# A transformer block with self- and cross-attention on one core: VectorE's remainders and statistics spread one to a beat, reciprocals of even units two beats later, the split of the contexts' keys on GpSimd

## The chip, the cores and the metric

The kernel runs on one NeuronCore of one Trainium2 chip. Five engines take part, each with its own in-order queue: TensorE (PE; PEld is its weight load), VectorE (DVE), ScalarE (ACT), GpSimd (POOL) and SyncE (SP), which here only issues DMAs. The metric is the device time of one execution in microseconds (us). A difference of 0.2% is about what a measurement of this kernel can tell.

## The reference

A block with 16 heads of 16 channels is computed for 16 batches of 256 tokens, width 256, in float32. Each batch has a condition vector and a context of 256 tokens.

```python
x_norm = modulate(_ln(x), shift_a, scale_a)
q, k, v = split(x_norm @ W_qkv + b_qkv)              # 16 heads of 16
x = x + gate_a * (softmax(q k^T * scale) v @ W_proj + b_proj)
q_c = _ln(x) @ W_qc + b_qc
k_c, v_c = split(_ln(context) @ W_kvc + b_kvc)
x = x + softmax(q_c k_c^T * scale) v_c @ W_cproj + b_cproj
x_norm2 = modulate(_ln(x), shift_m, scale_m)
x = x + gate_m * (gelu(x_norm2 @ W_mlp1 + b_mlp1) @ W_mlp2 + b_mlp2)
```

## The kernel before

**Units.** The attention is done in 32 units, one after the other. A spatial unit s*b* is the self-attention of batch *b*, a context unit c*b* its cross-attention. Units 0 to 4 are s0 to s4; then they alternate, s5, c0, s6, c1, up to s15 and c10 (units 5 to 26), so that odd units are spatial and even ones are contexts; units 27 to 31 are c11 to c15. The MLP of all batches follows.

**Beats.** A unit takes 8 beats, one for each pair of head groups (`beat(n, k)`, k from 0 to 7). In each beat PE makes the scores `s` of unit n+1 (4 matmuls into the two banks of `s`), DVE takes their row maxima (`mxs<-s`, one TENSOR_REDUCE of 128x1024), PE makes the transposed scores `st` of unit n, and ACT takes their exponential (`pt<-st`). There is one buffer of `s`: the next beat's `s` matmuls wait for this beat's reduce. Between these four steps, the beats carry the preparation of later units and the rest of earlier ones. All engines keep the order in which the program is written (`InOrder`, L51; every instruction has this line in the profile).

**What is prepared.** Matmuls work on float32 values split into a high part and a remainder. For the unit n+2 (`q2` in the code) the keys `K` and the queries `Q` are finished in beats 0 and 4: ACT writes the high part (`h_k`, `h_q`; `h_kc`, `h_qc` for contexts) from the PSUM tile, DVE the remainder (`l_k`, `l_q`, `l_kc`, `l_qc`: two instructions of 128x256, one for each half f), and SP sends both to where the scores read them (`big`), the high part in two DMAs and the remainder in one, 256 KB each. For the unit n+4 the layer norm is made: `stats` (two bn_stats, `st_s` or `st_c`), `rstd` (two bn_aggr on DVE, `mv`, then two short POOL instructions, `rs`) and `apply` (two POOL instructions, `xn`). For the unit n+3 (`q3`) the normalized tokens are transposed (`psT`) and projected.

**What is finished.** The unit n-1 (`p1`) has its sums `S` pulled (SP), inverted (`recip`, DVE), written to DRAM (`spread`: `rd<-S`) and read back broadcast (`back`: `R<-rd`); POOL multiplies in beat 0 of the next unit (`norm`, `U`), splits the product (`xTh_a`, `xTl_a`), and PE projects it (`ps_P`) in beats 3 and 5.

**The three banks `tr`.** Five or six PSUM tiles of a unit share three banks (the tag `tr` in `ps_gen`). They are asked for in this order: `ps_q` (queries of n+2) and `psT` (tokens of n+3) in beat 1, the output tile `o` of the first half in beat 2, `ps_k` or `ps_kc` (keys of n+3) in beat 5, in beat 5 also a second `psT_q` where unit n+3 is a context (its queries come from the updated x), and `o` of the second half in beat 6. A tile gets a bank when the last reader of an earlier tile is done: for `ps_q` this is the remainder `l_q` on DVE, for `psT` of beat 1 an instruction of beat 3, for `o` the copy to `oT` on ACT (in beat 5, and in beat 0 of the next unit). The first matmul into the new tile waits for that reader.

**Beat 5 on PE.** Written order: `s` with the first pieces of `psT_q` between its halves, `st`, then the key projection of n+3 (`ps_kc`) and the output projection (`ps_P`) in turn, matmul by matmul, each on one half of the array's rows; then the next beat's `s`. This happens 16 times with a `psT_q`: in units 3, 5, ... 23, where the unit n+2 is spatial, and in units 24 to 28, where it is a context.

Of the kernel before, what the change touches and what calls it, by code (L numbers as in the profile page):

```python
# [10 lines left out]
F32 = mybir.dt.float32  # L11
F32R = mybir.dt.float32r
# [9 lines left out]
def pixart_block(  # L22
# [488 lines left out]
    def to_stack(W, src, bias, dst, which, name):  # L511
# [24 lines left out]
        def low():  # L536
            if name == "k0":
                gap(work, 64, "gap_l")
            o.lo = work.tile([P, KC, N], F32R, tag="qkl", name=f"l_{name}", bufs=3)
            if name == "k0":  # L540
                gap(work, 576, "gap_mx")
            for f in range(KC):
                DVE.scalar_tensor_tensor(o.lo[:, f], o.ps[:, f * N:(f + 1) * N], bias[f], o.hi[:, f],
                                         ALU.add, ALU.subtract)
# [609 lines left out]
    def spare(n, gate=True):  # L1154
        p1, _, p3 = (v and v.post for v in map(unit, (n - 1, n - 2, n - 3)))
        if p3 and not p3.added:
            p3.add()
        if p1 and gate:
            p1.gate()

    def beat(n, k):
# [11 lines left out]
        late = lc and lc.b in (0, B - 1)  # L1173
        if k == 0 and q2:
            q2.K.high()
            q2.K.send_high()
# [27 lines left out]
        if k == 0:  # L1204
# [6 lines left out]
            if q2:  # L1211
                q2.K.low()
                q2.K.send_low()
# [4 lines left out]
        elif k == 1:  # L1218
# [6 lines left out]
            if lx:  # L1225
                if lx.b in (0, B - 1):
                    lx.ln[1].steps[0]()
                lx.ln[1].steps[1]()
                lx.ln[1].steps[2]()
        elif k == 2:  # L1230
# [7 lines left out]
            if ls:  # L1238
                ls.ln[0].steps[0]()
            elif prev:  # L1240
                p1.recip()
                p1.spread()
            if not (q3 and q3.kind == "c"):
                spare(n)
        elif k == 3:
# [12 lines left out]
            if q3 and q3.kind == "s":  # L1258
                q3.T[0].low()
            if prev and ls:  # L1260
                p1.recip()
                p1.spread()
            if lx and n == nu - 4:
                lx.T[0].parts[2]()
        elif k == 4:
# [5 lines left out]
            if q2:  # L1271
                q2.Q.low()
                q2.Q.send_low()
# [4 lines left out]
            if ls:  # L1278
                ls.ln[0].steps[1]()
                ls.ln[0].steps[2]()  # L1280
                ls.ready = True
        elif k == 5:
# [4 lines left out]
            if lc:  # L1287
                lc.ln[0].steps[1]()
                lc.ln[0].steps[2]()
                lc.ready = True  # L1290
# [147 lines left out]
```

## Time and profile before

| what | value |
|---|---|
| median of 3 runs | 725.73 us (725.42 to 726.89) |
| the profiled execution | 722.92 us |
| its span, first to last instruction | 721.1 us |
| first and last row maximum (`mxs<-s`) of the 32 units | 18.9 and 524.2 us |
| one row maximum, 128x1024 | 1221 ns, 252 of them |
| mean granted TensorE clock | 1.000 |

The profile of one execution gives the busy time of each engine, waits (who waited for whom), groups of like instructions with the mean duration of one, and a timeline whose rows read: start in us, duration in us, engine, line, operation, tile written and tiles read, partitions x elements, number of instructions in the row, and in brackets the engine's idle time before the row with what ended it. Matmuls are pipelined and their ends are modelled, so rows of PE overlap and a busy PE may be waiting in part.

### The profile page before, as it was taken

Reading aid. Unit: us, or ns where it says so; the run is one execution under the profiler, and the core shown is the slowest. Engines: PE = TensorE matmul, PEld = TensorE weight load, DVE = VectorE, ACT = ScalarE, POOL = GpSimd, SP = SyncE. Lnnn points to the kernel's source line nnn. Section 1 sums busy time; section 2 is a strip of 40 time slices with the busy share of each in tenths; the row PEclk is TensorE's granted clock in tenths of the full one; section 3 lists DMA queues with packets and bytes.
Section 4 is the critical chain, followed back from the end, with each engine's and each line's share of the span. In section 5 each row is a group of like instructions: output and inputs, shape, how many; then the busy total and the mean of one; then the engine's idle time right before and its main releaser. Section 6 shows DMA issues by size and latency. Waiting matters only on the chain.

```text
span 721.1 us, 23569 instructions
## 1 busy us (share of the span) xinstructions
PE 704.2 (98%) x9359; PEld 600.5 (83%) x9359; DVE 566.5 (79%) x895; ACT 551.0 (76%) x956; POOL 520.5 (72%) x519
## 2 busy tenths in 40 slices
PE   9999999999999999999999999999999999999997
PEld 8777788788877878787778787877779999999997
DVE  5878888988888888778888888888765777777753
ACT  5677888888888888787888888877867677676661
POOL 7665778886776768676686698987766988676552
PEclk9999999999999999999999999999999999999999
DMA  7465455354545536454545556545332223223122
GB/s 238 166 201 200 151 185 194 134 182 167 176 161 186 177 138 189 160 177 150 184 164 193 172 186 204 166 153 206 102 104 87 89 59 89 69 66 86 48 59 74
DMA packets 82921, 106.22 MB, mean 147 GB/s; under 512 B 18970, under 2 KB 45916, under 8 KB 82812
## 3 DMA queue, kind: packets, MB, share of 16 engines
q1 hardware_dynamic: 81916, 104.37, 44.0%
q8 instruction: 74, 1.21, 0.8%
q10 hardware_dynamic: 896, 0.35, 0.2%
q14 instruction: 35, 0.29, 0.1%
HBM read 35.89 MB, written 8.98 MB: 62 GB/s over the span
## 4 chain that ended last, share of the span: by engine, by line
PE 75%; DVE 13%; DMA 4%; issue 2%; POOL 2%; SPq 2%; ACT 1%; POOLq 0%; ACTq 0%; DVEq 0%
PE s L51 18%; PE st L51 13%; PE ph L51 12%; PE o L51 10%; DVE mxs L51 9%; PE ps_kc L51 3%; PE ps_q L51 3%; PE ps_P_s L51 2%; PE ps_k L51 2%; PE ps_v_c L51 2%; SPq L51 2%; PE ps_qc L51 2%; DMA x<-in_x_dram 2%; PE ps_v_s L51 1%; DMA U_s<-oT 1%
## 5 line engine op out<-in xcount | busy, mean ns | idle before, releaser
L51 DVE TENSOR_REDUCE mxs<-s 128x4 f32<-128x1024 f32 x252 | 307.6, 1221 | 65.3 <-PE s L51 60.0
L51 ACT ACTIVATE pt<-st 128x1024 f32<-128x1024 f32 x256 | 262.6, 1026 | 74.6 <-PE st L51 70.4
L51 PE MATMUL s<-big 63*128 63x256 f32 x1008 | 132.9, 322 | 10.9 <-DVE mxs L51 4.3
L51 PE MATMUL o<-pt,v 128*32 128x256 f32 x2048 | 141.6, 384 | 0.0
L51 PEld LDWEIGHTS s<-big 63*128 63x128 f32 x1008 | 82.4, 185 | 70.4 <-DVE mxs L51 62.3
L51 PE MATMUL st<-big 64*128 64x256 f32 (+1 forms) x1040 | 112.4, 285 | 0.3 <-ACT pt L51 0.2
L51 PE MATMUL ph<-xTh_m,wself 128*128 128x256 f32 x512 | 99.6, 280 | 0.0
L51 POOL TENSOR_TENSOR hl<-hf,hh 128x512 fp32r<-128x512 f32 x60 | 80.2, 1354 | 19.2 <-ACT hh L51 19.2
L51 PEld LDWEIGHTS st<-big 64*128 64x128 f32 (+1 forms) x1040 | 85.7, 186 | 3.0 <-ACT pt L51 1.4
L51 PEld LDWEIGHTS o<-pt,v 128*32 128x32 f32 x2048 | 67.0, 109 | 21.7
L51 PEld LDWEIGHTS ph<-xTh_m,wself 128*128 128x128 f32 x512 | 81.9, 188 | 1.2 <-issue 0.4
L51 PE MATMUL ph<-xTl_m,wself 128*128 128x256 f32 x256 | 70.9, 277 | 0.0
L51 ACT ACTIVATE hf<-ph,bT 128x256 f32<-128x256 f32 x112 | 47.0, 473 | 20.6 <-PE ph L51 20.3
L51 ACT ACTIVATE hh<-ph,bT 128x256 fp32r<-128x256 f32 x112 | 47.0, 473 | 19.3 <-PE st L51 8.3
L51 PEld LDWEIGHTS ph<-xTl_m,wself 128*128 128x128 f32 x256 | 48.1, 188 | 0.0
L51 DVE TENSOR_SCALAR xn_m<-x,mv_m,rs_m 128x256 f32<-128x256 f32 x28 | 33.5, 1236 | 15.0 <-POOL rs_m L51 15.0
L51 PE MATMUL s<-big,hh 128*128 128x256 f32 x256 | 45.2, 277 | 0.0
L51 POOL TENSOR_SCALAR rs_c<-mv_c 128x2 f32<-128x2 f32 x16 | 3.6, 228 | 53.5 <-DVE mv_c L51 53.3
L51 POOL TENSOR_SCALAR xn_q<-x,mv_q,rs_q 128x256 f32<-128x256 f32 x32 | 38.9, 1226 | 1.7
L51 POOL TENSOR_SCALAR xn_c<-c,mv_c,rs_c 128x256 f32<-128x256 f32 x32 | 38.9, 1226 | 1.7
L51 PE MATMUL st<-big,hh 128*128 128x256 f32 x224 | 39.5, 276 | 0.0
L51 PEld LDWEIGHTS s<-big,hh 128*128 128x128 f32 x256 | 38.7, 188 | 0.0
(225 smaller groups left out, 2156.9 us busy)
## 6 DMA issues: line engine op xcount, KB each, us to landing
big<-h_k SPq DMA_DIRECT2D x32, 256.0 KB
big<-h_kc SPq DMA_DIRECT2D x32, 256.0 KB
big<-h_qc SPq DMA_DIRECT2D x32, 256.0 KB
big<-h_q SPq DMA_DIRECT2D x30, 256.0 KB
big<-l_k SPq DMA_DIRECT2D x16, 256.0 KB
g<-gd SPq DMA_DIRECT2D x16, 256.0 KB
U_s<-oT SPq DMA_DIRECT2D x32, 128.0 KB
R_s<-rd_s SPq DMA_DIRECT2D x16, 256.0 KB
```

The source lines that it names most:

```text
L51: i = f(*a, **k)
```

## The change

Five things are moved, all of them in `beat`, with two helpers new in `to_stack`.

1. Where the unit n+2 is spatial, the remainder of its keys is made one half in beat 0 and one half in beat 1, and sent in beat 1 (before: both halves in beat 0). The remainder of its queries is made one half in beat 4 and one in beat 5, and sent in beat 5 (before: beat 4).
2. Where the unit n+2 is a context (`by_pool`), ACT writes the keys whole (`y`, float32) in beat 0; POOL makes high part and remainder from it in beat 2 (a copy and a subtraction of 128x512); SP sends all three in beat 4. DVE has no part in it. The remainder of its queries is made in beat 5, both halves, and sent there.
3. The two bn_stats of a spatial unit n+4 are made in beats 2 and 3 (before: both in beat 2).
4. Where the unit n+4 is no spatial one (even n, and all n from 22 on), reciprocal and `spread` of unit n-1 go from beat 2 to beat 4.
5. Where the unit n+4 is a context, its `rstd` and `apply` go from beat 5 to beat 2, and POOL's part of them stands behind the split of item 2.

```diff
+        def low_of(f):
+            if f == 0 and name != "k0":
+                o.lo = work.tile([P, KC, N], F32R, tag="qkl", name=f"l_{name}", bufs=3)
+            DVE.scalar_tensor_tensor(o.lo[:, f], o.ps[:, f * N:(f + 1) * N], bias[f], o.hi[:, f],
+                                     ALU.add, ALU.subtract)
+
+        def whole():
+            o.y = work.tile([P, KC, N], F32, tag="y", name=f"y_{name}", bufs=1)
+            for f in range(KC):
+                ACT.activation(o.y[:, f], o.ps[:, f * N:(f + 1) * N], AF.Identity, bias=bias[f])
+
+        def split_pool():
+            o.hi = work.tile([P, KC, N], F32R, tag="qkh", name=f"h_{name}", bufs=3)
+            o.lo = work.tile([P, KC, N], F32R, tag="qkl", name=f"l_{name}", bufs=3)
+            POOL.tensor_copy(o.hi, o.y)
+            POOL.tensor_tensor(o.lo, o.y, o.hi, ALU.subtract)
...
+        by_pool = q2 and q2.kind == "c"
         if k == 0 and q2:
-            q2.K.high()
-            q2.K.send_high()
+            if by_pool:
+                q2.K.whole()
+            else:
+                q2.K.high()
+                q2.K.send_high()
...
             if prev:
                 av_part(prev, 3)
                 p1.pull_sums(1)
-            if q2:
-                q2.K.low()
-                q2.K.send_low()
+            if q2 and not by_pool:
+                q2.K.low_of(0)
...
+            if q2 and not by_pool:
+                q2.K.low_of(1)
+                q2.K.send_low()
         elif k == 2:
...
             if ls:
-                ls.ln[0].steps[0]()
-            elif prev:
-                p1.recip()
-                p1.spread()
+                ls.ln[0].stat(0)
+            if lc:
+                lc.ln[0].steps[1](False)
             if not (q3 and q3.kind == "c"):
                 spare(n)
+            if by_pool:
+                q2.K.split_pool()
+            if lc:
+                lc.ln[0].pow()
+                lc.ln[0].steps[2]()
+                lc.ready = True
         elif k == 3:
...
+            if ls:
+                ls.ln[0].stat(1)
             if prev and ls:
                 p1.recip()
                 p1.spread()
...
             if cur:
                 av_part(cur, 1)
-            if q2:
-                q2.Q.low()
-                q2.Q.send_low()
+            if by_pool:
+                q2.K.send_high()
+                q2.K.send_low()
+            if prev and not ls:
+                p1.recip()
+                p1.spread()
...
                 ls.ready = True
+            if q2 and not by_pool:
+                q2.Q.low_of(0)
         elif k == 5:
             exps()
             rest_of()
             if cur:
                 o_out(cur, 0)
-            if lc:
-                lc.ln[0].steps[1]()
-                lc.ln[0].steps[2]()
-                lc.ready = True
+            if q2:
+                for f in range(not by_pool, 2):
+                    q2.Q.low_of(f)
+                q2.Q.send_low()
             if prev:
                 p1.back()
```

DVE, unit 17, beats 3 to 5, before (`l_q` is the remainder of the queries of unit 19, `mv_s` the aggregated statistics of unit 21; a row that ends in x3 stands for three instructions):

```order
L51 TENSOR_REDUCE mxs<-s 128x4 [waits PE_49]
L51 RECIPROCAL S_c_5916<-S_c_5916 128x32 [waits DMAHW5_49,DMAHW2_49]
L51 TENSOR_REDUCE mxs<-s 128x4 [waits PE_49]
L51 SCALAR_TENSOR_TENSOR l_q_6150<-ps_q_5995,bqkv,h_q_6126 128x256 [waits DMAHW6_49,Activation_49]
L51 SCALAR_TENSOR_TENSOR l_q_6150<-ps_q_5995,bqkv,h_q_6126 128x256
L51 BN_AGGR mv_s_6156<-st_s_6079 128x2 [waits DVE_49,Pool_49]
L51 BN_AGGR mv_s_6156<-st_s_6079 128x2 [waits DVE_49]
L51 TENSOR_REDUCE mxs<-s 128x4 [waits PE_49] x3
```

The same place now:

```order
L51 BN_STATS st_s_6086<-x_5965 128x6
L51 RECIPROCAL S_c_5923<-S_c_5923 128x32 [waits DMAHW5_49,DMAHW2_49]
L51 TENSOR_REDUCE mxs<-s 128x4 [waits PE_49]
L51 BN_AGGR mv_s_6159<-st_s_6086 128x2 [waits DVE_49,Pool_49]
L51 BN_AGGR mv_s_6159<-st_s_6086 128x2 [waits DVE_49]
L51 SCALAR_TENSOR_TENSOR l_q_6168<-ps_q_6000,bqkv,h_q_6133 128x256 [waits Activation_49,Pool_49]
L51 TENSOR_REDUCE mxs<-s 128x4 [waits PE_49]
L51 SCALAR_TENSOR_TENSOR l_q_6168<-ps_q_6000,bqkv,h_q_6133 128x256
L51 TENSOR_REDUCE mxs<-s 128x4 [waits PE_49] x2
```

The second half of `l_q` has moved behind the reduce of beat 5; it is the last reader of the bank `ps_q`.

PE, the same beat, now (the order on PE is the same as before; `ps_kc` lies in the bank that `ps_q` had, before and now, and its first matmul waits for the second half of `l_q`):

```order
L51 MATMUL s<-big_79 128x256 x2
L51 MATMUL st<-big_82 128x256 [waits Activation_49]
L51 MATMUL st<-big_82 128x256 x3
L51 MATMUL ps_kc_6170<-xTh_c_6097,wkch 128x256 [waits DVE_49]
L51 MATMUL ps_P_s_6104<-wself,xTh_as_5996 128x256
L51 MATMUL ps_kc_6170<-xTh_c_6097,wkcl 128x256
```

The rows of PE have not moved, but the instruction that the fourth waits for has.

SP, unit 18, from the end of beat 2, before (`rd_s` and `R_s` belong to unit 17, `h_qc` and `l_qc` to unit 20; the DMAs of `h_kc` and `l_kc` stand nine, eight and six rows further up, in beats 0 and 1):

```order
L51 DMA rd_s_6407<-S_s_6252 128x32 [waits DMAHW1_49,DMAHW0_49,DVE_49]
L51 DMA big_82<-h_qc_6456 32x4x512 [waits Activation_49]
L51 DMA big_82<-h_qc_6456 32x4x512 [waits DMAHW2_49]
L51 DMA big_82<-l_qc_6480 32x4x512 [waits DMAHW3_49,DVE_49]
L51 DMA R_s_6531<-rd_s_6407 128x1x512 [waits DMAHW4_49,DMAHW0_49,Pool_49]
```

The same place now:

```order
L51 DMA big_82<-h_qc_6467 32x4x512 [waits DMAHW5_49,PE_49,Activation_49]
L51 DMA big_82<-h_qc_6467 32x4x512 [waits DMAHW6_49]
L51 DMA big_82<-h_kc_6416 32x4x512 [waits DMAHW7_49,Pool_49]
L51 DMA big_82<-h_kc_6416 32x4x512 [waits DMAHW0_49]
L51 DMA big_82<-l_kc_6417 32x4x512 [waits DMAHW1_49,Pool_49]
L51 DMA rd_s_6495<-S_s_6259 128x32 [waits DMAHW2_49,DVE_49]
L51 DMA big_82<-l_qc_6535 32x4x512 [waits DMAHW3_49,DVE_49]
L51 DMA R_s_6539<-rd_s_6495 128x1x512 [waits DMAHW4_49,DMAHW2_49]
```

The three DMAs of the keys now stand between those of the queries' high part and `rd_s`, and `rd_s` behind `h_qc`.

More of the change, by code (lines that the diff above doesn't have):

```diff
@@ L538, in low @@
                 gap(work, 64, "gap_l")
-            o.lo = work.tile([P, KC, N], F32R, tag="qkl", name=f"l_{name}", bufs=3)
-            if name == "k0":
+                o.lo = work.tile([P, KC, N], F32R, tag="qkl", name=f"l_{name}", bufs=3)
                 gap(work, 576, "gap_mx")
             for f in range(KC):
-                DVE.scalar_tensor_tensor(o.lo[:, f], o.ps[:, f * N:(f + 1) * N], bias[f], o.hi[:, f],
-                                         ALU.add, ALU.subtract)
+                low_of(f)
+        def low_of(f):
[9 more added lines that the diff above has]
+            o.hi = work.tile([P, KC, N], F32R, tag="qkh", name=f"h_{name}", bufs=3)
+            o.lo = work.tile([P, KC, N], F32R, tag="qkl", name=f"l_{name}", bufs=3)
+            POOL.tensor_copy(o.hi, o.y)
+            POOL.tensor_tensor(o.lo, o.y, o.hi, ALU.subtract)
+        o.low_of, o.whole, o.split_pool = low_of, whole, split_pool
         def low_pool():
```

## The prediction

> **What bounds the kernel now.** I read the page first: busy times, granted clock, and the chain of work that ended last.
>
> ```profile
> PE 704.2 (98%) x9359; PEld 600.5 (83%) x9359; DVE 566.5 (79%) x895; ACT 551.0 (76%) x956; POOL 520.5 (72%) x519
> PEclk9999999999999999999999999999999999999999
> PE 75%; DVE 13%; DMA 4%; issue 2%; POOL 2%; SPq 2%; ACT 1%; POOLq 0%; ACTq 0%; DVEq 0%
> ```
>
> PE carries three quarters of the chain and DVE an eighth. PE's 98% does not mean that nothing can be gained or lost there: the ends of matmuls are modelled. The waits show the loop between the two engines.
>
> ```profile
> PEld s L51 <- DVE mxs L51: 62.3, 122, 1.2
> DVE mxs L51 <- PE s L51: 60.0, 116, 1.4
> DVE S_s L51 <- DMA S_s<-oT: 8.0, 10, 2.0
> DVE S_c L51 <- DMA S_c<-oT: 3.7, 3, 2.0
> DVE st_s L51 <- DMA x<-in_x_dram: 3.6, 5, 1.6
> ```
>
> (Total us, times, longest.) PE waits for the row maximum before it may write the next scores, and DVE waits for the scores: each beat goes once round this loop. What delays either lengthens the beat and is not made up later. The last three rows are DVE waiting for a DMA in front of a reduce. Unit 17, beats 4 to 6, on DVE and then on PE:
>
> ```profile
> 309.10 1.22 DVE L51 TENSOR_REDUCE mxs<-s 128x4 f32<-128x1024 f32 x1 [0.34 <-PE s L51]
> 310.24 0.87 DVE L51 SCALAR_TENSOR_TENSOR l_q<-ps_q,bqkv,h_q 128x256 fp32r<-128x256 f32 x2
> 311.23 1.22 DVE L51 TENSOR_REDUCE mxs<-s 128x4 f32<-128x1024 f32 x1
> 313.05 1.22 DVE L51 TENSOR_REDUCE mxs<-s 128x4 f32<-128x1024 f32 x1 [0.60 <-PE s L51]
> ```
>
> ```profile
> 310.96 0.45 PE L51 MATMUL st<-big 64*128 64x256 f32 x4
> 311.20 0.35 PE L51 MATMUL ps_P_s<-wself,xTh_as 64*128 64x256 f32 x1
> 311.26 0.28 PE L51 MATMUL ps_kc<-xTh_c,wkch 64*128 64x256 f32 x1
> ...
> 312.31 0.27 PE L51 MATMUL ps_P_s<-wself,xTl_as 64*128 64x256 f32 x1
> 312.50 0.39 PE L51 MATMUL s<-big 63*128 63x256 f32 x2
> ```
>
> An instruction behind a reduce starts 1.14 us after the reduce's start (310.24 against 309.10). The reduce of beat 5 ends at 312.45, and `s` of beat 6 starts 0.05 later. Between 311.20 and 312.50 PE is full with `ps_kc` and `ps_P`: this block just fits under the reduce.
>
> **The change, part by part.**
>
> *The remainder of the queries a beat later.* The second half of `l_q` now stands behind the reduce of beat 5, and it frees the bank that `ps_kc` takes in that same beat, on PE ahead of the next `s`. Nothing can pass on PE.
>
> ```profile
> L51 DVE SCALAR_TENSOR_TENSOR l_q<-ps_q,bqkv,h_q 128x256 fp32r<-128x256 f32 x32 | 13.9, 476 | 1.3 <-ACT h_q L51 1.3
> 312.45 0.58 ACT L51 COPY oT<-o 128x512 f32<-128x512 f32 x1
> ```
>
> The half ends at 311.23 + 1.14 + 0.48 = 312.85; with the 0.05 that PE needed after the reduce, `ps_kc` starts at 312.90 instead of 311.26, 1.64 later. The block and `s` move with it (312.50 to 314.14), and the reduce of beat 6, which had no slack but its wait for `s`, too. Another bank would not help: `psT_q` has one, and `o` holds the third until its copy to `oT` ends at 312.45 + 0.58 = 313.03. In units 3, 5, ... 23, this is 11 x 1.64 = 18.0 us. In units 24 to 28 both halves stand behind the reduce: 0.87 (the pair's row) in place of 0.48, so 2.03 each, 5 x 2.03 = 10.2. Sum **+28.2**. Lower bound 16 x 1.5 = 24, if PE's starts are modelled 0.1 off; upper bound 31, if the wait costs 0.2 more at each place. In the other even units `ps_k` takes the bank of `psT`, free since beat 3, and nothing waits.
>
> *Reciprocals two beats later, statistics split.* What DVE loses on DMAs in front of a reduce is seen at units 14, 16, 18 and 20:
>
> ```profile
> 256.16 1.22 DVE L51 TENSOR_REDUCE mxs<-s 128x4 f32<-128x1024 f32 x1
> 258.90 0.35 DVE L51 RECIPROCAL S_s<-S_s 128x32 f32<-128x32 f32 x1 [1.52 <-DMA S_s<-oT]
> 259.17 1.16 DVE L51 TENSOR_REDUCE mxs<-s 128x4 f32<-128x1024 f32 x1
> ...
> 291.30 0.35 DVE L51 RECIPROCAL S_s<-S_s 128x32 f32<-128x32 f32 x1 [1.51 <-DMA S_s<-oT]
> ...
> 320.94 1.22 DVE L51 TENSOR_REDUCE mxs<-s 128x4 f32<-128x1024 f32 x1
> 324.12 0.35 DVE L51 RECIPROCAL S_s<-S_s 128x32 f32<-128x32 f32 x1 [1.95 <-DMA S_s<-oT]
> 324.39 1.16 DVE L51 TENSOR_REDUCE mxs<-s 128x4 f32<-128x1024 f32 x1
> ...
> 353.71 1.22 DVE L51 TENSOR_REDUCE mxs<-s 128x4 f32<-128x1024 f32 x1
> 355.51 0.35 DVE L51 RECIPROCAL S_s<-S_s 128x32 f32<-128x32 f32 x1 [0.57 <-DMA S_s<-oT]
> 355.78 1.22 DVE L51 TENSOR_REDUCE mxs<-s 128x4 f32<-128x1024 f32 x1
> ```
>
> A wait of 0.57 leaves this beat at 2.07 (355.78 - 353.71); 1.52 makes it 3.01, 1.95 makes it 3.45. So a wait costs what it has above 0.57: 0.95 + 0.94 + 1.38 = 3.3 us for the three. Two beats later the sums have landed. The `S_c` waits give at most 3.7 - 3 x 0.57 = 2.0 and at least nothing, as a wait of the tail counts among them: I take 1.0. Of the `st_s` waits (3.6) the split saves only the second bn_stats behind the wait, about 0.37 (half of a pair of 0.75) where it reached a reduce: two places, 0.7, between 0 and 1.9. Sum **-5.0**, from -3 to -9 (with all of `S_s`).
>
> *DVE's other moves.* Taking `l_kc` away and halving `l_k` in beat 0 costs and gains nothing: in the next beat PE weaves transposes between the scores, and DVE waits for them. In even units the 0.87 of `l_qc` only goes from one reduce to the next. Layer norm of contexts in beat 2: two short bn_aggr in a beat that lost its reciprocal, 0.
>
> *The split on GpSimd.* POOL gets a copy and a subtraction more, 16 times.
>
> ```profile
> L51 POOL CAST xTh_as<-U_s 128x512 fp32r<-128x512 f32 x16 | 9.8, 610 | 1.1
> L51 POOL TENSOR_TENSOR xTl_c<-y_c,xTh_c 128x512 fp32r<-128x512 f32 x15 | 19.2, 1283 | 5.7 <-ACT y_c L51 5.7
> 289.76 1.28 POOL L51 TENSOR_TENSOR xg<-x,g 128x512 f32<-128x512 f32 x1
> 296.80 0.23 POOL L51 TENSOR_SCALAR rs_c<-mv_c 128x2 f32<-128x2 f32 x1 [5.76 <-DVE mv_c L51]
> 300.34 1.28 POOL L51 TENSOR_TENSOR U_s<-U_s,R_s 128x512 f32<-128x512 f32 x1
> ```
>
> 0.61 + 1.28 = 1.89 us go into the 5.76 us in which POOL waits for `mv_c` in unit 16: cost 0. If that cover were gone, `U_s` would come 1.89 later. [...]
>
> *DMAs.* In even units the keys' three DMAs now go out ahead of `rd`, `l_qc` and `R`, which the next unit needs.
>
> ```profile
> 295.33 1.22 DVE L51 TENSOR_REDUCE mxs<-s 128x4 f32<-128x1024 f32 x1
> 295.45 0.53 SPq L51 DMA_DIRECT2D big<-l_qc  x1
> 296.11 0.67 SPq L51 DMA_DIRECT2D R_s<-rd_s  x1
> 300.35 0.49 PE L51 MATMUL s<-big 63*128 63x256 f32 x4
> 302.67 0.58 SPq L51 DMA_DIRECT2D x<-in_x_dram  x1
> 306.62 0.75 DVE L51 BATCH_NORM_STATS2 st_s<-x 128x6 f32<-128x256 f32 x2 [0.57 <-DMA x<-in_x_dram]
> ```
>
> `l_qc` went out 0.12 after the reduce of beat 5 began and is needed 5.02 after it; now it goes out at 1.14 + 0.87 + 0.05 = 2.06. With the 3.95 that `x` took (306.62 - 302.67), 256 KB too, it would be 1.0 late; at 2.9 or less it is in time. `R_s` moves by the same 1.94, and behind it stands POOL's `U_s`. Ten even units (4, 6, ... 22): between 0 and 10 x (1.0 + 1.94) = 29. Most DMAs landed faster than that `x`, on which DVE waited, so I stay near the lower end: **+4**.
>
> **The sum**: 28.2 - 5.0 + 4 = +27 us. The profiled execution took 722.9 (span 721.1), 2.8 below the median; the differences carry over, so 725.7 + 27 = **753 us**.
>
> **The rivals.**
>
> *Late DMAs count in full in even units.* For it: two rows later in the queue, and lateness of `R` stops POOL, whose `xn_q` the transposes of beat 5 read. Against it: POOL sat idle 5.76 us there. At 1.5 us in ten units, 15 in place of 4: 764 us; with 29, 778.
>
> *The pause hides, and the kernel is faster.* Place: beat 5, `ps_kc`. If the block behind the bank could run later without holding `s` (it is needed only by beat 7), only the 5.0 us gained would remain: 720.7 us. It decides from 5.0 / 16 = 0.31 us for each place downward. Against it: `s` at 312.50 follows the block on an in-order queue, and 1.64 is five times 0.31.
>
> *Half of it hides*, because beats 6 and 7 hold slack which I do not see: 14 - 5 + 4 = +13, 739 us. Against it: the row at 313.05 waits for `s` alone.
>
> *The clock falls.* PE now stands still for up to 2 us at 16 places; if each pause halved the clock for the next two beats (3.9 us), it would cost 16 x 3.9 = 62 us, 815 us. Against it: in unit 18 a beat of 3.45 us left the granted clock at 9 tenths or more in every slice. [...]
>
> *The change doesn't do what it says*: the reciprocals still wait in beat 4. Then 3 to 4 us of the gain are missing, 757: inside the range.
>
> **Chances.** The wait at `ps_kc` in full, DMAs nearly hidden: 0.70, 745 to 760. Late DMAs in full: 0.18, above 760. Half hidden: 0.06. Pause hidden: 0.04. Clock: 0.02. The range 743 to 770 leaves out the hidden cases, the clock and a third of the late DMAs, under 0.2. A difference of 0.2% (1.5 us) is about what a measurement of this kernel can tell; slower by more than that: 0.95; faster: 0.04; same: 0.01.
>
> **What would show it.** In the profile after: a wait of PE or its weight load on `l_q` and `l_qc`, 16 times, about 1.6 (2.0 in units 24 to 28), some 28 us in all; `ps_kc` starting after the reduce of beat 5 has ended; beats 6 of these units near 3.5 us in place of 1.8; no wait of `S_s` or `S_c` on its DMA before unit 30; POOL's gap before `rs_c` gone; few waits of `s` on `l_qc` or `l_kc`. I am wrong if beat 6 stays at 1.8 us, or if beat 0 of odd units or POOL's `U_s` lengthens by over 1 us.

## The result, and the profile after

The changed kernel takes **796.88 us** (median of 4 runs, 795.12 to 798.39), the kernel before, measured with it, 725.58 (723.17 to 726.89): ratio 1.0986, 95% interval 1.0947 to 1.1025. It is slower by 71 us; the prediction had 753, slower by 27. The profiled execution's span is 796.6 us against 721.1, a difference of 75.5, as the longest of the changed kernel's four executions was profiled.

The page of the changed kernel: busy times, granted clock, and the chain of work that ended last.

```profile
PE 731.9 (92%) x9359; PEld 618.0 (78%) x9359; DVE 557.7 (70%) x863; ACT 555.3 (70%) x956; POOL 550.4 (69%) x551
PEclk9999999999999999999999988999999999999999
PE 57%; DVE 15%; POOL 12%; DMA 7%; issue 5%; SPq 2%; ACT 1%; POOLq 0%; ACTq 0%; DVEq 0%
```

Three things stand out. TensorE's share of the chain fell from 75 to 57%, and GpSimd (2 to 12%) and the DMAs (4 to 7%) took its place. The engines have nearly the same instructions to do, in a longer span. And the granted clock of TensorE is no longer full: two slices of 40 show an 8, and the mean is 0.969.

Its waits (total us, times, longest):

```profile
DVE mxs L51 <- PE s L51: 147.5, 158, 3.9
...
PEld ps_kc L51 <- DVE l_q L51: 18.5, 11, 1.7
PE ps_kc L51 <- DVE l_q L51: 16.3, 11, 1.5
...
DVE st_s L51 <- DMA x<-in_x_dram: 13.4, 8, 4.2
...
ACT y_c L51 <- POOL l_kc L51: 9.7, 4, 2.5
...
PEld ps_kc L51 <- DVE l_qc L51: 5.0, 5, 2.1
PE s L51 <- DMA big<-l_qc: 5.0, 4, 1.6
...
PE psT_q L51 <- ACT y_c L51: 3.2, 4, 0.9
...
PE ps_kc L51 <- POOL xTl_c L51: 1.7, 3, 1.2
```

The wait at the bank is there as forecast, 11 times on `l_q` and 5 times on `l_qc`. Four other kinds are new or larger: `x` in front of the bn_stats (3.6 before), the first scores on `l_qc`, ACT's `y_c` on GpSimd's `l_kc`, and `ps_kc` on GpSimd's `xTl_c`. VectorE's wait for the scores, 60.0 before, is 147.5: that is where all of them end.

The timeline of the changed kernel, unit 15 from the reduce of beat 5 to that of beat 6, on DVE:

```profile
306.46 1.22 DVE L51 TENSOR_REDUCE mxs<-s 128x4 f32<-128x1024 f32 x1 [0.38 <-PE s L51]
307.60 0.47 DVE L51 SCALAR_TENSOR_TENSOR l_q<-ps_q,bqkv,h_q 128x256 fp32r<-128x256 f32 x1
309.83 1.23 DVE L51 TENSOR_REDUCE mxs<-s 128x4 f32<-128x1024 f32 x1 [1.75 <-PE s L51]
```

The same on PE:

```profile
306.19 0.45 PE L51 MATMUL st<-big 64*128 64x256 f32 x4
308.13 0.38 PE L51 MATMUL ps_kc<-xTh_c,wkch 64*128 64x256 f32 x1 [1.49 <-DVE l_q L51]
...
309.37 0.42 PE L51 MATMUL s<-big 63*128 63x256 f32 x4
```

The half of `l_q` behind the reduce ends at 308.07, `ps_kc` starts 0.06 later, the block takes 1.24, and the reduce of beat 6 starts 3.37 after that of beat 5. Before, it was 1.82: 1.55 more, where the prediction had 1.64.

This is a clean place. At others the same beat is longer, and the granted clock tells why. Stretches of 3.41 us of the changed kernel around beat 5 of units 3, 7 and 11 (columns: us, busy time of PE, PEld, DVE, ACT and POOL with the number of instructions, PEclk, DMA share, GB/s):

```profile
95.05:98.46 3.41, 1.93 (x34) 1.73 (x32) 1.66 (x3) 1.50 (x2) 3.13 (x5) 1.00 0.45 169
98.46:101.88 3.42, 3.42 (x62) 2.85 (x60) 2.19 (x2) 2.92 (x5) 1.19 (x2) 1.00 0.73 248
166.73:170.15 3.42, 1.85 (x29) 1.13 (x22) 2.83 (x6) 2.52 (x4) 3.34 (x4) 1.00 0.47 165
170.15:173.56 3.41, 3.41 (x34) 3.32 (x34) 0.71 (x1) 0.59 (x1) 3.13 (x4) 0.50 0.49 159
...
235.00:238.41 3.41, 1.84 (x30) 1.57 (x28) 2.25 (x6) 1.93 (x3) 3.24 (x5) 1.00 0.46 162
238.41:241.83 3.42, 3.42 (x42) 3.08 (x42) 1.23 (x1) 1.34 (x2) 2.66 (x3) 0.50 0.68 212
```

After a stretch in which PE was busy 1.85 or 1.84 us, the next one has half the clock (PEclk 0.50, "half clock" below), and here that lasts 3.41 us. After the one with 1.93 the clock is full (1.00). The kernel before has no such stretch: its least busy one in the units, with the long beat of unit 18, is

```profile
322.13:325.54 3.41, 2.50 (x40) 1.95 (x32) 1.46 (x4) 3.11 (x7) 2.83 (x3) 1.00 0.56 204
```

In the changed kernel there are 12 such places in the 32 units (3.413 us long, two of them 6.827), and they begin on one grid: 238.41 - 170.15 = 68.26 = 20 x 3.413.

Where the 75.5 us of the span went: the first row maximum starts 2.0 later (20.8 against 18.9; it lies between 18.9 and 20.9 in the profiles of kernels with the same prologue, so this is not the change's), the tail behind the units is 0.1 longer, and the rest, summed over all units by the beat that ends with the reduce, is

| beat | 0 | 1 | 2 | 3 | 4 | 5 | 6 | 7 |
|---|---|---|---|---|---|---|---|---|
| us more than before | 14.5 | 1.0 | 1.2 | 2.5 | 2.4 | 3.5 | 39.5 | 8.9 |

By cause, worked out from the same rows: the bank's wait 11 x 1.55 + 5 x 1.96 = 26.9 (1.96 as in unit 28, where nothing else disturbs it); half clock 18.0 (what beats 6 and 7 of ten units have above that, and two more beats, less the next item); `ps_kc` on `xTl_c` in units 23 to 27, 3.9 (what beat 6 has there above the bank's wait in the run below that kept the clock full); the first scores of a unit late, 14.5; `x` late, 7.3; 4.0 in beat 5 of units 24 to 27, where `y_c` waits; the waits of `S` gone, -4.9; the rest in small pieces.

### The profile page after: what moved, and what is told of

Read it like the earlier page. It is cut to its first block, busy times and chain, and to the rows that moved or that the text cites. A ratio compares the mean times of both kernels' runs of the same rounds, so it can differ in the third digit from the quotient of the medians.

```text
span 796.6 us, 23521 instructions
## 1 busy us (share of the span) xinstructions
PE 731.9 (92%) x9359; PEld 618.0 (78%) x9359; DVE 557.7 (70%) x863; ACT 555.3 (70%) x956; POOL 550.4 (69%) x551
## 4 chain that ended last, share of the span: by engine, by line
PE 57%; DVE 15%; POOL 12%; DMA 7%; issue 5%; SPq 2%; ACT 1%; POOLq 0%; ACTq 0%; DVEq 0%
PE s L51 15%; DVE mxs L51 11%; PE st L51 10%; PE ph L51 9%; PE o L51 8%; PE ps_kc L51 4%; PE ps_v_c L51 2%; SPq L51 2%; POOL xn_c L51 2%; PE ps_k L51 1%; PE ps_q L51 1%; DMA x<-in_x_dram 1%; POOL xn_q L51 1%; PE ps_v_s L51 1%; POOL l_kc L51 1%
## 5 line engine op out<-in xcount | busy, mean ns | idle before, releaser
L51 DVE TENSOR_REDUCE mxs<-s 128x4 f32<-128x1024 f32 x252 | 307.9, 1222 | 150.1 <-PE s L51 147.5
L51 PE MATMUL s<-big 63*128 63x256 f32 x1008 | 134.0, 324 | 28.6 <-DVE mxs L51 9.7
L51 PEld LDWEIGHTS s<-big 63*128 63x128 f32 x1008 | 86.3, 192 | 89.1 <-DVE mxs L51 55.7
L51 PE MATMUL o<-pt,v 128*32 128x256 f32 x2048 | 147.2, 395 | 0.0
L51 PE MATMUL st<-big 64*128 64x256 f32 (+1 forms) x1040 | 116.9, 293 | 4.3 <-ACT pt L51 4.3
L51 PEld LDWEIGHTS st<-big 64*128 64x128 f32 (+1 forms) x1040 | 89.9, 194 | 7.9 <-ACT pt L51 6.3
L51 PEld LDWEIGHTS o<-pt,v 128*32 128x32 f32 x2048 | 70.0, 113 | 23.1 <-issue 1.4
L51 POOL TENSOR_TENSOR U_s<-U_s,R_s 128x512 f32<-128x512 f32 x16 | 20.6, 1290 | 84.7 <-DMA R_s<-rd_s 34.6
L51 ACT ACTIVATE hh<-ph,bT 128x256 fp32r<-128x256 f32 x112 | 47.2, 475 | 19.1 <-PE st L51 9.0
L51 PE MATMUL ps_kc<-xTh_c,wkch 64*128 64x256 f32 x128 | 35.6, 306 | 20.2 <-DVE l_q L51 16.3
L51 PEld LDWEIGHTS ps_kc<-xTh_c,wkch 64*128 64x128 f32 x128 | 25.4, 199 | 23.6 <-DVE l_q L51 18.5
L51 POOL TENSOR_TENSOR U_c<-U_c,R_c 128x512 f32<-128x512 f32 x15 | 19.4, 1291 | 31.0 <-DMA R_c<-rd_c 15.7
L51 PE MATMUL ps_P_s<-wself,xTh_as 64*128 64x256 f32 x256 | 40.2, 290 | 0.0
```

What stands on the lines that cost most here:

```text
L51: i = f(*a, **k)
```

## The experiments

Each run is compared with the kernel before on the same chip; the ratio is that of the two, with its 95% interval.

### The bank, and the clock behind it

**The remainder of the queries alone.** The kernel before with item 1's queries and the last sentence of item 2.

```diff
-            if q2:
-                q2.Q.low()
-                q2.Q.send_low()
...
+            if q2 and q2.kind == "s":
+                q2.Q.low_of(0)
         elif k == 5:
...
+            if q2:
+                for f in range(q2.kind == "s", 2):
+                    q2.Q.low_of(f)
+                q2.Q.send_low()
```

> The kernel before with one part of the change alone: the remainder of the queries a beat later (one half in beat 4 and one in beat 5 for spatial units, both in beat 5 for contexts, sent in beat 5). Theory (bank and clock): 16 waits, 11 x 1.55 + 5 x 1.96 = 27 us, about 20 us of half clock behind them, 3 us of late DMAs: 726 + 50 = 776 us, mean granted clock about 0.97. Rival (the low clock comes with the late keys and the shared buffer of the rest of the change): 726 + 27 + 3 = 756 us, clock above 0.99.

Measured 761.48 us, ratio 1.0526 (1.0478 to 1.0573), mean clock 0.991. Of its waits:

```profile
PE ps_kc L51 <- DVE l_q L51: 16.2, 11, 1.5
...
PE ps_kc L51 <- DVE l_qc L51: 9.4, 5, 1.9
```

The 16 waits are there in full: beat 6 is longer by 1.53 to 1.57 in nine places and by 1.94 or 1.95 in three; in the other four half clock is added. Only 4 stretches of half clock follow, 6.1 us, not 20: the time lies between the two expectations. Where the pauses stand alone, the clock stayed full in 12 of the 16 places.

**The queries of spatial units back in beat 4**, all else as changed.

```diff
             if q2 and not by_pool:
-                q2.Q.low_of(0)
+                q2.Q.low()
+                q2.Q.send_low()
...
-            if q2:
-                for f in range(not by_pool, 2):
-                    q2.Q.low_of(f)
-                q2.Q.send_low()
+            if by_pool:
+                q2.Q.low()
+                q2.Q.send_low()
```

> The changed kernel with one part undone: where the unit n+2 is spatial, both halves of the remainder of its queries stand in beat 4 again and are sent there; contexts stay as changed. Theory (the bank's wait, and the clock that halves behind it): the 11 waits of ps_kc on l_q go, 11 x 1.55 = 17 us, and with them the stretches of half clock in units 5 to 23 that follow them, about 11 us: 797 - 28 = 769 us, mean granted clock about 0.98, half clock left in units 24 to 27. Rival (late transfers make the rest of the loss, the low clock costs nothing of its own): only the 17 us come back, 780 us.

Measured 767.46 us, ratio 1.0611 (1.0554 to 1.0668). The clock is 0.978 in the profiled execution, the longest of the four by 6.6 us, and 0.986 to 0.988 in the others. As the theory had it: 29 us come back for 17 us of waits. One stretch of half clock is left in units 5 to 22, and it follows a wait for `x`, not one at the bank.

**All queries back in beat 4.** The same, and `if q2:` in place of `if q2 and not by_pool:`, with nothing left in beat 5.

> The changed kernel with the remainder of all queries, of contexts too, back in beat 4 with its DMA. Theory (bank and clock): beside the 28 us of the spatial units, 5 x 1.96 = 10 us of waits on l_qc and 8 us of half clock in units 24 to 27 go, and some 12 us at beat 0 of odd units, where the first scores waited for l_qc; reciprocal and l_qc now share beat 4 of even units, which costs about 0.4 x 12 = 5: 797 - 28 - 10 - 8 - 12 + 5 = 744 us, no half clock. Rival (late transfers of the keys' high part and remainder hold the first scores, not l_qc, and the clock costs nothing): 797 - 17 - 10 + 5 = 775 us.

Measured 769.46 us, ratio 1.0621 (1.0584 to 1.0657), clock 0.982. The theory missed by 25 us and the rival by 6; the rival is right in its first half, that the late transfers of the keys hold the first scores. The five waits on `l_qc` are gone, and nothing is gained: in units 24 to 27 beats 5 and 6 are still 1.9 and 2.2 longer than before, now because of ACT's `y_c` and GpSimd's `xTl_c`; and the first scores of odd units are still late by 10 us in all, although `l_qc` is made early again. So `l_qc`'s wait at the bank and GpSimd's lateness hide one another there, and the late first scores are not due to the beat in which `l_qc` is made.

**TensorE kept busy in the pause.** The transposed scores `st` of beat 5 are made three times instead of once in the 16 units.

```diff
         in_turn(*t)
+        if k == 5 and mid:
+            for _ in range(2):
+                in_turn(*[t_part(units[n], k, par) for par in range(2)])
         later.append(lambda: exp(units[n], k))
```

> The changed kernel with work added: in beat 5 of the 16 units where ps_kc waits for the bank, the 4 matmuls of the transposed scores are issued three times instead of once (the same values into the same bank), so that TensorE is busy about 1 us of the pause. Theory (the clock halves when TensorE is busy less than about 1.9 of 3.4 us): the clock stays full there, and of the 22 us of half clock 17 to 20 come back although there is more work: 778 us (774 to 784), mean granted clock above 0.99. Rival (the clock falls for another reason than TensorE's own pause): 797 us or more, clock 0.97.

Measured 777.77 us, ratio 1.0730 (1.0683 to 1.0776): with 128 matmuls more the kernel is 19.1 us faster than the changed one. Span and mean granted clock of the profiled execution, the fastest of the four (the others have 0.986 to 0.990):

```profile
core 0: 772.8 us, clock 0.993
```

Its timeline on PE, unit 7, beat 5:

```profile
164.44 0.92 PE L51 MATMUL st<-big 64*128 64x256 f32 x12
166.38 0.39 PE L51 MATMUL ps_kc<-xTh_c,wkch 64*128 64x256 f32 x1 [1.02 <-DVE l_q L51]
```

The pause is 1.02 where unit 15 of the changed kernel had 1.49, `ps_kc` starts no earlier behind the reduce, and beat 6 has its 1.56 more than before and nothing else; in the changed kernel it had 2.70. Within the units half clock is left at two places, behind a wait for `x` in unit 5 and in unit 25. So here the low clock went with TensorE's idle share: the mean is 0.993 with the added matmuls and 0.969 without them. What the low clock cost of its own is probably less than the 19.1: behind the first row maximum the two profiled executions lie 22 us apart, of which 14.5 are in beats 1 and 5 to 7, where the half clock was, and 8.2 in beats 0 and 3, where DMAs are waited for and which this edit does not reach directly (beat 4 is 0.7 longer).

### The keys of the contexts

**The split on GpSimd alone** (item 2 without its queries; the first diff), and **the changed kernel without it** (the second, with the queries' remainder late as changed).

```diff
+            if by_pool:
+                q2.K.split_pool()
         elif k == 3:
...
+            if by_pool:
+                q2.K.send_high()
+                q2.K.send_low()
             if q2:
                 q2.Q.low()
```

```diff
-        by_pool = q2 and q2.kind == "c"
+        by_pool = False
...
+                if ctx:
+                    q2.K.low_of(1)
+                    q2.K.send_low()
```

> The kernel before with the split of the contexts' keys on GpSimd alone (sent in beat 4); reciprocals, queries and layer norm as before. Theory (late keys): 10 us at beat 0 of odd units, 6 us on x, 8 us in units 24 to 27, where ACT waits for the buffer y and TensorE for ACT: 726 + 24 = 750 us. Rival (the prediction's: the split hides in GpSimd's idle time, and the DMAs cost 4 us): 730 us.

> The changed kernel with the split of the contexts' keys undone: ACT and DVE make high part and remainder in beat 0 as before, and the three DMAs go out in beats 0 and 1; all else as changed, the queries' remainder late too. Theory (the late keys hold SP's queue): the first scores of odd units start in time (10 us), the waits of bn_stats on x go (8 us), the shared buffer y in units 24 to 27 too (4 us), and some half clock with them (7 us): 797 - 29 = 768 us. Rival (the late DMAs come from the queries' remainder and the reciprocals, which stay): 797 - 4 = 793 us.

Measured 758.14 us, ratio 1.0442 (1.0400 to 1.0485), and 762.89 us, 1.0502 (1.0471 to 1.0533). The split alone costs 32 us, and without it the changed kernel is 34 us faster. The prediction had 4. In the trace of the split alone 21.9 us lie in beat 0, 5.3 in beat 1 (half clock behind late first scores), 8.7 in beat 5 of units 24 to 27 and 3.1 in beat 6; beat 3 wins 4.3.

Two things come with the split: GpSimd's 1.89 us, and DMAs that go out in beat 4 instead of 0. The next two runs were to tell them apart and did not.

**Split a beat earlier, keys sent in beat 3**, and the same with **`y` in the tile of `l_kc`** (`o.y = o.lo.bitcast(F32)`).

```diff
                 p1.pull_values(1)
+            if by_pool:
+                q2.K.split_pool()
...
         elif k == 3:
...
+            if by_pool:
+                q2.K.send_high()
+                q2.K.send_low()
```

> As the run with the split on GpSimd alone, but the split stands one beat earlier (beat 1, right behind U's products) and the three DMAs of the keys go out in beat 3, ahead of those of the queries' high part instead of behind them. Theory (SP sends one DMA after the other, and the three of the keys held back the queries' remainder and R behind them): the 20 us at beat 0 of odd units fall to 3, with some 6 us of half clock; units 24 to 27 keep their loss by the buffer y: 758 - 23 = 735 us. Rival (the transfers themselves contend, whatever their order): 750 us or more.

> As the run with split and DMAs early, and ACT writes the keys whole into the tile of l_kc (GpSimd subtracts in place) instead of the single buffer y, which the tokens' copy y_c needs in units 24 to 27. Theory (the shared buffer held ACT there until GpSimd was done, and TensorE behind ACT): another 6 to 9 us come back: 727 us, about as before, so that the split's own work on GpSimd does hide. Rival (GpSimd's 1.89 us are late in every unit): 735 us or more, like the run beside it.

Measured 753.78 us, ratio 1.0385 (1.0337 to 1.0434), and 756.12 us, 1.0436 (1.0392 to 1.0479): both theories miss (735 and 727), and both runs lie where the rivals put them. That does not decide for the rivals. The keys' three DMAs now stood ahead of `h_qc` instead of behind, but still ahead of `l_qc`, which went out as late as in the run before; beat 0 lost 25.5 and 28.0. That was a fault of the experiment: what it moved was not what had to move. It shows one thing: with the split a beat earlier, beat 5 of units 24 to 27 loses 0.9 in place of 8.7, with the shared buffer as well as without, so it was GpSimd's lateness that held `y_c`, and another buffer adds nothing.

**Late DMAs without the work, and the work without late DMAs.** First, the kernel before with the keys' three DMAs in beat 4 and nothing else moved:

```diff
             q2.K.high()
-            q2.K.send_high()
+            if not ctx:
+                q2.K.send_high()
...
                 q2.K.low()
-                q2.K.send_low()
+                if not ctx:
+                    q2.K.send_low()
...
                 av_part(cur, 1)
+            if ctx:
+                q2.K.send_high()
+                q2.K.send_low()
             if q2:
                 q2.Q.low()
```

> The kernel before, with nothing moved but the three DMAs of the contexts' keys: ACT and DVE make high part and remainder in beat 0 as before, SP sends them in beat 4, where the changed kernel does, ahead of l_qc, rd or R of that unit. GpSimd has no part in it. Theory (the late DMAs are what the split costs: SP issues 1.9 us more ahead of l_qc, and six transfers of 256 KB fall into the same few us): nearly all that the split on GpSimd alone cost in units 0 to 23, about 20 us, half clock in it: 746 us. Rival (GpSimd's 1.9 us, which came late to U and xn, are what it costs): 728 us.

Second, the split on GpSimd, but first in beat 0, and the DMAs in beat 1:

```diff
                 p1.pull_sums(1)
-            if q2:
+            if by_pool:
+                q2.K.split_pool()
+            elif q2:
                 q2.K.low()
                 q2.K.send_low()
...
         elif k == 1:
...
+            if by_pool:
+                q2.K.send_high()
+                q2.K.send_low()
```

> The split of the contexts' keys on GpSimd alone, but first in beat 0, ahead of U, and the three DMAs in beat 1, about where the kernel before has them. Theory (late DMAs are the cost, GpSimd's work hides): the first scores of odd units start in time again; U and what hangs on it come 1.9 us later, which costs at most 0.3 us in 15 units: 726 to 731 us. Rival (GpSimd's work is late in every unit): 745 us or more.

Measured **752.80 us**, ratio 1.0404 (1.0369 to 1.0439), and **727.69 us**, 1.0043 (1.0021 to 1.0065). The late DMAs cost 28.6 us without any work on GpSimd, nearly what the split did; in the trace, beats 0 and 1 lose 34.0 and beat 3 wins 4.9, as the waits of `S` go. The work without late DMAs costs 3 us in all: 5.4 us are lost in units 25 to 28, where `psT_q` waits for `xn_q`, 0.9 at unit 4, nearly nothing in units 5 to 13 and 19 to 24, and some 4 us are won at units 14 to 18 and 29, of which more below. SP's queue in unit 20, before and with the late DMAs, first before:

```profile
358.07 0.33 SPq L51 DMA_DIRECT2D rd_s<-S_s  x1
358.45 1.22 SPq L51 DMA_DIRECT2D big<-h_qc  x2
359.77 0.55 SPq L51 DMA_DIRECT2D big<-l_qc  x1
360.43 0.67 SPq L51 DMA_DIRECT2D R_s<-rd_s  x1
```

The same with the late DMAs, and the first scores of unit 21 on PE:

```profile
368.11 0.33 SPq L51 DMA_DIRECT2D rd_s<-S_s  x1
368.54 1.23 SPq L51 DMA_DIRECT2D big<-h_qc  x2
369.83 1.26 SPq L51 DMA_DIRECT2D big<-h_kc  x2
371.13 0.61 SPq L51 DMA_DIRECT2D big<-l_kc  x1
371.84 0.56 SPq L51 DMA_DIRECT2D big<-l_qc  x1
372.51 0.67 SPq L51 DMA_DIRECT2D R_s<-rd_s  x1
...
376.94 0.50 PE L51 MATMUL s<-big 63*128 63x256 f32 x4 [2.08 <-DMA big<-l_qc]
```

`l_qc` goes out 3.73 us behind `rd_s` (371.84 - 368.11) where it went 1.70 (359.77 - 358.07), and it is used 5.10 after its issue, where the trace of before has it landed 2.4 after. With `R_s`, seven transfers of 256 KB go out within 4 us, four before.

The later place in the queue is not enough by itself. In the run with the queries' remainder alone, `l_qc` went out 2 us later too, and beat 0 of units 7 to 21 lost nothing. With the late DMAs it lands 4.8 and 4.7 behind the start of the reduce of beat 5 in units 6 and 8, where the first scores of before start at 5.0: just in time. Where it is late, the trace's records of completion, in which each of these DMAs of 256 KB comes in 16 parts, show which part is late. In unit 20, 15 parts of `l_qc` had landed 2.54 after its issue, and the last one landed after 4.96; a fetch of instructions (16 KB on queue 8 of the page, a DMA as well) had started 1.30 after the issue. Before, the same is seen in unit 18 (last part 4.90 after the issue, fetch at 0.77), and there the earlier issue nearly covers it (beat 0 of unit 19 has 0.3 more than in five of the other runs). Over the 16 units that send an `l_qc`, the last part took more than 3.4 us in 11 with the late DMAs, in 4 before, and in 2 with the queries' remainder alone, where it is these two that cost: beat 0 of units 5 and 23 lost 1.2 and 1.8. So the later place takes the slack, and a late last part then holds the first scores, 16.1 us in 8 waits of PE on `l_qc` (in units 12 and 14 a still later issue, 3.0 and 3.7 behind the reduce's start where the others have 2.1 to 3.0). In unit 18 of the late-DMA run all five transfers from the second `h_qc` to `l_qc` have a last part 1.3 to 2.1 us behind the rest; no run parts crowd, place and fetch further.

Behind late first scores half clock is seen as at the bank, here behind a stretch with 1.36 us of work; the late-DMA run, around the first scores of unit 5:

```profile
110.20:113.61 3.41, 1.36 (x24) 1.19 (x23) 1.68 (x3) 1.87 (x3) 1.12 (x1) 1.00 0.68 202
113.61:117.03 3.42, 3.42 (x29) 1.93 (x31) 2.01 (x3) 1.45 (x2) 2.16 (x3) 0.50 0.50 138
```

On GpSimd the split's copy and subtraction took 0.61 to 0.63 and 1.27 to 1.30 us (`h_kc` and `l_kc` of the changed kernel, 16 each), on VectorE each of the two instructions of `l_kc` 0.47 to 0.48 before. What the longer time costs is shown by the run with the work alone: 3 us.

### The layer norm of the contexts

**Item 5 alone** (aggregation, `rs_c` and `xn_c` in beat 2).

```diff
+            if lc:
+                lc.ln[0].steps[1](False)
             if not (q3 and q3.kind == "c"):
                 spare(n)
+            if lc:
+                lc.ln[0].pow()
+                lc.ln[0].steps[2]()
```

> The kernel before with the layer norm of the contexts in beat 2 alone (rs_c and xn_c on GpSimd stand ahead of xTl_c). Theory (GpSimd's queue in units 23 to 27): ps_kc waits for xTl_c there, 5 x 2 = 10 us: 736 us. Rival (the prediction's: it costs nothing): 726 us.

Measured 733.50 us, ratio 1.0123 (1.0083 to 1.0164). Of its waits:

```profile
PE ps_kc L51 <- POOL xTl_c L51: 7.2, 5, 1.6
```

In units 23 to 27 unit n+3 is a context too, whose `xTl_c` GpSimd makes in beat 4. `rs_c` and `xn_c` now stand ahead of it, and the last four matmuls of `ps_kc` wait. Beat 6 is longer by 1.0 to 1.7 there, 7.7 us in five units; the other units differ from before by about 1 us at most.

The single parts add up: 5.3 + 4.4 + 1.2 = 10.9% against 9.9% for the whole (queries, split and layer norm; the other items were not run alone); in units 24 to 27 their waits overlap.

### The reciprocals

**Two beats later in units 4 to 22, with room made on DVE** (one half of `l_qc` of these units in beat 5), and bn_stats split; then **three beats later**, `l_qc` left in beat 4.

```diff
-            elif prev:
+            elif prev and not room:
                 p1.recip()
                 p1.spread()
...
+            if room:
+                p1.recip()
+                p1.spread()
+                q2.Q.low_of(0)
```

> The kernel before with the reciprocals of units 4 to 22 (even ones) two beats later and the two bn_stats of spatial units in two beats; to make room for the reciprocal on DVE, one half of l_qc of these units stands behind the reduce of beat 5, where no bank waits for it; keys, layer norm and all other queries as before. Theory (the waits of S_s cost what they have above 0.57 us, and a remainder sent later is in time when the keys were sent early): 726 - 4 = 722 us, 0.5 per cent faster. Rival (the later l_qc and R hold the first scores or GpSimd as in the changed kernel): 726 to 735 us.

> The kernel before with the reciprocals of units 4 to 22 (even ones) in beat 5 (three beats later) and the two bn_stats in two beats; nothing else is moved, so the queries' remainder goes out as before. Theory (S_s waits cost 3.3 us, and the run with room lost them again through l_qc sent later): 726 - 3.5 = 722 us. Rival (R, which now goes out later, holds GpSimd's U and what hangs on it): 726 us or more.

Measured 727.15 us, ratio 1.0017 (1.0000 to 1.0034), and 730.64 us, 1.0091 (1.0058 to 1.0123). In both the waits of `S_s` are gone at units 14, 16 and 18, for the 0.95, 0.93 and 1.38 us that the prediction had. In both something else takes it back: 4.7 us at beat 0 in the first, where `l_qc` is late; in the second, `x` in front of the bn_stats. SP's queue at the end of unit 18 in the second:

```profile
331.13 0.33 SPq L51 DMA_DIRECT2D rd_s<-S_s  x1
334.12 0.68 SPq L51 DMA_DIRECT2D R_s<-rd_s  x1
...
338.42 0.58 SPq L51 DMA_DIRECT2D x<-in_x_dram  x1
```

And of its waits:

```profile
DVE st_s L51 <- DMA x<-in_x_dram: 13.3, 9, 2.8
```

`R_s` reads what `rd_s` wrote and stands on SP until that has landed, 2.7 us after its issue ended (334.12 - 331.46); all rows behind, `x` too, go out later. Here, too, a last part counts: 15 parts of `rd_s` had landed 1.41 after its issue, the last one 2.94 after it.

**The sums ahead of the keys.** In the runs with the keys' DMAs moved away, the waits of `S_s` had gone although the reciprocal stayed in beat 2. So the reciprocal is left where it was, and only one row on SP moves: the second DMA of `S` ahead of the two of `h_kc`; then the same in all units.

```diff
         if k == 0 and q2:
             q2.K.high()
-            q2.K.send_high()
+            if not behind:
+                q2.K.send_high()
...
                 p1.pull_sums(1)
+            if behind:
+                q2.K.send_high()
```

> The kernel before with one row moved on SP: in units before a context, the second DMA of the sums S goes out ahead of the two DMAs of the keys' high part instead of behind them; reciprocals stay in beat 2, all else as before. Theory (the reciprocals waited because S stood behind 512 KB of keys): the waits of S_s go, 3.3 us at units 14, 16 and 18 and up to 1 us more in the tail, and the keys sent 0.6 us later cost nothing: 724.2 - 3.7 = 720.5 us, 0.5 per cent faster than before. Rival (S is late for another reason, so that only the place of the reciprocal helps): 724 us, no change.

> The same in all units, spatial ones too. Theory (the same reason holds for S_c and in the first units): at most another 1 us, 719.5 to 721 us. Rival (the keys of spatial units have no slack of 0.6 us, or S_c was never late in front of its reduce): 721 to 725 us.

Measured **718.47 us**, ratio **0.9924 (0.9904 to 0.9944)**, and 721.57 us, 0.9957 (0.9940 to 0.9974). The first is faster than both kernels, 0.8% faster than the one before. Its reciprocals of spatial units no longer wait at all, as the group's row shows (busy us, mean ns, idle us before):

```profile
L51 DVE RECIPROCAL S_s<-S_s 128x32 f32<-128x32 f32 x16 | 5.5, 342 | 0.0
```

Its timeline on DVE in unit 18, where the reciprocal follows its reduce at once and had waited 1.95 before:

```profile
318.32 1.23 DVE L51 TENSOR_REDUCE mxs<-s 128x4 f32<-128x1024 f32 x1
319.46 0.34 DVE L51 RECIPROCAL S_s<-S_s 128x32 f32<-128x32 f32 x1
```

Units 14, 16, 18 and 29 give 0.94, 0.94, 1.38 and 1.12 us. These 4.4 are the move's; the medians lie 6.1 apart (4.1 to 7.0 by the interval). Unit 1 is another 1.1 shorter in the profiled execution, but nothing is moved there, and it differs by as much between other runs. Moving the sums in spatial units too gains the same there and loses 0.9 at unit 5 and 1.9 in the tail of the profiled execution.

## Why the prediction was right and wrong

- **The bank's wait, +28.2: right.** 16 waits, 1.55 for 1.64 and 1.96 for 2.03, 26.9 us in the trace; the run with this part alone shows them undisturbed.
- **The clock, forecast at nothing with a chance of 0.02: the step that failed most.** "In unit 18 a beat of 3.45 us left the granted clock at 9 tenths or more" was taken for a bound, and single pauses of up to 2 us were set against it. In the traces the half clock goes with the busy time of TensorE in a stretch of 3.41 us: in the changed kernel it followed 12 of the 16 stretches with at most 1.93 us of work, and none with more. That beat's stretch had 2.50 us, well above the 1.93 that is the most after which the full clock fell in any run, so it bounded nothing. The half clock cost 18.0 us by the beats; the run that kept TensorE busy gave 19.1 back, of which about two thirds can be placed where the half clock was (14.5 of 22), so that the two figures agree so well is partly luck. The forecast's 62 us for this rival was too much: it took 16 falls at 3.9 us, and there were 12 at about 1.5.
- **Late DMAs, "I stay near the lower end: +4": failed.** Late first scores cost 14.5 us in the changed kernel, and the late keys alone 28.6 with the half clock they bring. The bounds (0 to 29) held it; the choice between them was wrong, for it took the landing time of a DMA from a trace in which the keys had gone 5 to 6 us earlier, and took the slow landings for exceptions: the `x` with 3.95 was one whose last part came 1.0 behind the others. It also counted units 4 to 22 only; in the run with the late DMAs alone, units 25 to 30 lose 12.7 of the 28.6.
- **The split on GpSimd, cost 0: half right.** Its work nearly hides in units 4 to 22, as the run with the work alone shows (0.9 us at unit 4, 0.3 at unit 19; it stands in beat 0 there, not in beat 2). But the gap of 5.76 us was read from unit 16; in units 24 to 27 GpSimd has `xn_q` and `xTl_c` to make, and 4.0 us follow from `y_c` there, with part of the 3.9 from `xTl_c`.
- **Layer norm in beat 2, 0: failed.** Only DVE's two short instructions were costed, not the two of GpSimd ahead of `xTl_c`: 7.7 us alone.
- **Reciprocals, -5.0: right in size, wrong in what it needs.** The waits went for 4.9 us in the changed kernel, but the late keys' DMAs alone remove them as well. Late `x` cost 7.3, more than they gave. Most of that is units 5 and 21 (4.2 us of wait at the longest). There 15 of the 16 parts of `x` had landed 2.88 and 3.03 after its issue, as elsewhere, and the last one only after 5.67 and 5.26, with an instruction fetch started 1.48 and 2.73 after the issue; the rest is a later issue.
- **The rivals.** Late DMAs in full (764 to 778) came nearest. With the clock's 18 us added to the upper end they reach the measured time, but by luck: the first scores cost 14.5, not 29, and `x`, layer norm and GpSimd make up the rest. That the pause hides was refuted by beat 6.

## What to carry to other kernels

Here the pauses on TensorE had two prices: their own length, 26.9 us, and half clock behind 12 stretches of 3.41 us in which TensorE was busy for 0.71 to 1.93 us, 18.0 us; ask the trace for the busy time in such stretches, not for the longest gap alone. When work moves, cost each queue that its parts stand in: here the work by itself lost 6 us, and the DMAs that went along, into a crowd of seven on an in-order queue, lost 34. Here a DMA that landed in time in other units had its slack eaten where its last part came 2 us late (`l_qc` of unit 20 with the late DMAs, 4.96 for 2.54 us): take the slowest landing of the trace, not the usual one. Where a wait for a DMA is to be removed, look first for what stands ahead of that DMA: one row moved on SP gave 0.8%, the reciprocal moved on DVE nothing.

## What the runs showed of the hardware

In the record of the changed kernel the 12 places of half clock in the units are 3.413 us long, two of them 6.827, and they begin 10, 30, 61, 68, 72, 82, 94, 100, 107, 113 and 119 times 3.413 us behind the first. Of the 154 stretches of this grid in the units that had the full clock, all 3 with TensorE busy for less than 1.64 us were followed by half clock, 9 of the 13 with 1.64 to 1.93, and none of the 138 with more. Over the records of the changed kernel and eleven of the others together, each on a grid of its own, these are all of 42, 22 of 47, and none; the other five have no stretch with less than 2.2 us of work, and no half clock in the units. What decides in between stays open; the ends of matmuls are modelled, so the busy time is itself uncertain. The longest pause of TensorE in the stretch with 1.84 us of work (235.00 to 238.41) was 1.48 us.

The late last part was counted for the DMAs into `big` and into `x` in the units that come in 16 parts. Where a 16-KB fetch of instructions started between 0.5 us before the issue and the landing of the fifteenth part, the last part came over 0.9 us behind the fifteenth in 58 of 117 cases in the traces of the kernel before and the changed one, and in 517 of 977 over all seventeen records; where no fetch did, in 3 of 256 and in 17 of 2136; where only an 8-KB fetch on queue 14 did, in 3 of 33 and in 23 of 335. So late last parts were seen together with fetches; that the fetch delays them was not shown, as no run moved a fetch.
